# Two layers on one core: the second layer's dense weights load into the first layer's expert space, and its first sequence is entered in the first layer's last turns

## The chip, the core and the metric

The kernel runs on one core of a Trainium2 chip. The metric is the device time of one execution in microseconds (us); lower is better. Five engines work side by side, each with its own queue of instructions in a fixed order: TensorE (PE: matrix products and transposes; its weight loads are listed as PEld), VectorE (DVE), ScalarE (ACT), GpSimd (POOL) and SyncE (SP, which issues DMA transfers). ACT and POOL issue DMA transfers too. An instruction waits until the instructions whose results or buffers it needs are done, and everything behind it in its engine's queue waits with it.

## The reference

The input is 8 sequences of 512 tokens with 256 features, all in 32-bit floats. Cut to what matters here:

```python
xn = layernorm(x)
x = x + recurrent(xn) + experts0(xn)     # layer 0
xn = layernorm(x)
x = x + attention(xn) + experts1(xn)     # layer 1

# recurrent: mixes of neighbouring tokens, projections r, k, v, g, w; a forward and a
#   backward recurrence over the 512 tokens; sigmoid gate, group norm (16 heads), * silu(g), @ Wo
# experts0: each token goes to its 2 best of 8 experts (hidden size 704)
# attention: x + global_latent_attn(rmsnorm(x)), then + local_gqa_attn(rmsnorm(x)), window of 64
# experts1: 16 experts (hidden size 64): of 4 groups the best 2, of these the best 4 experts;
#   all experts are computed for all tokens and weighted; plus a shared expert of hidden size 512
```

The experts of layer 1 with the shared expert make 12 dense parts of 128 hidden units.

## The kernel before

The program is written as Python generators. A scheduler class, `Turns`, holds the running generators and advances each by one step per turn; a step ends at a `yield`. PE, DVE, ACT and SP execute their instructions in exactly the order in which this Python code issues them. Only POOL's order is chosen by the framework. So the order of everything around the change follows from how many `yield`s each generator has passed.

**Layer 0** (L239 to L808). After the norm, the routing and `place()` (slots of all tokens), the main loop is `scans`, in 64 turns over sequence, half of the features and group of values. For each group, DVE does one product (L688), four recurrences (L699, L703: two forward, two backward) and one product with r (L708), and PE sums over the keys (L714, `ys`). Beside `scans` run:

- `projections(b + 1)`, which prepares the next sequence.
- `ending(b, c, y, z, x)` for each finished half: gate (L734), centring product `yc` (L737), square (L740), variance (L747), root (L753, ACT), reciprocal (L755, DVE), widening (L758, ACT), transposes `rs` (L763, PE), z (L765, L766 on DVE, L767 on POOL); after the second half the output products `o` (L777), the sum x (L782) and the write of `after[b]` (L785, SP).
- `scatter`, then `experts`: 39 chunks of 256 slots. POOL fetches each chunk's weights; the results go to `outs` in DRAM (L472, L473).

The tiles of `experts` are in the pools `ew`, `h0` and `ex`; those of `projections`, `scans` and `ending` are in the pool `rw`; all of them close at the end of layer 0.

**Layer 1** (L811 to L1325) begins with the loads of all its weights on ACT's queue (L820 to L843; `w1` is the 12 dense parts, 384 KB each). Its own `Turns` then runs:

- `attentions`: 16 blocks in the order g0, g1, l0, g2, l1, ... (g is global, l is local attention; the number is the sequence). In each: scores (L1159, PE), exponential (L1167, ACT), mask (L1173, DVE), sums `o` (L1187, PE), and `divided` with the output projection. These give the turns.
- `heads_of(n)`: queries, keys and values of block n (L1001 to L1125), with rotary steps and norms on DVE.
- `entry(b)` (L891 to L994): loads `after[b]` into `acc`, gathers each token's two expert rows from `outs` (L903, POOL) and sums them (L911, DVE), norm (L919 to L926), transposes (L858), router logits (L945, PE), the choice of experts on DVE (L959 to L983, through `chosen`, L228 to L236), and the weights `cT` (L987), written to `cd` in DRAM.
- `ffn(b)` (L1254 to L1316): for each of 12 parts the products `g` and `u` (L1261, PE) and `h` (L1293 on ACT; L1296, L1279, L1281 on DVE; `cb` is a row of `cd`, loaded by SP), and after each six parts the products `y` (L1307). It starts once `entry(b)` is done.

The start of layer 1 in the kernel before:

```python
turns.add(
    then(*(heads_of(n) for n in range(len(BLOCKS)))),
    then(*(entry(b) for b in range(B))), then(*(ffn(b) for b in range(B))),
)
for _ in attentions(turns):
    turns.turn()
```

So `heads_of(0)` and `ffn(0)` wait for `entry(0)`, and the first score waits for `heads_of(0)`.

Of the kernel before, what the change touches and what calls it, by code (L numbers as in the profile page):

```python
# [26 lines left out]
F32 = mybir.dt.float32  # L27
# [9 lines left out]
P = 128  # L37
# [128 lines left out]
def two_layers(ctx: ExitStack, tc: tile.TileContext, a: dict, out: bass.AP):  # L166
# [6 lines left out]

    cst = const.tile([P, FIRST_L1], F32, name="cst")
# [6 lines left out]
    act_e.dma_start(wg0, a["wg0"])  # L181

# [38 lines left out]
    def chosen(dst, s, n, k, tri, tmp, tag, tags=None):  # L221

        rows = s.shape[1]
        tags = tags or (f"gt{n}", f"eq{n}")
        gt = tmp.tile([P, rows, n, n], F32, tag=tags[0], name=f"gt{n}_{tag}", bufs=1)
        eq = tmp.tile([P, rows, n, n], F32, tag=tags[1], name=f"eq{n}_{tag}", bufs=1)
        other, own = bc(s, 2, n), bc(s, 3, n)
        vec_e.tensor_tensor(gt, other, own, ALU.is_gt)  # L228
        vec_e.tensor_tensor(eq, other, own, ALU.is_equal)
        vec_e.tensor_tensor(  # L230
            eq.rearrange("p r i j -> p r (i j)"), eq.rearrange("p r i j -> p r (i j)"),
            bc(tri, 1, rows), ALU.mult,
        )
        vec_e.tensor_tensor(gt, gt, eq, ALU.add)
        vec_e.tensor_reduce(dst, gt, AX.X, ALU.add)
        vec_e.tensor_scalar(dst, dst, float(k), None, ALU.is_lt)  # L236


    with ExitStack() as l0:  # L239
# [3 lines left out]
        ew = l0.enter_context(tc.tile_pool(name="ew", bufs=2))  # L243
        hpool = l0.enter_context(tc.tile_pool(name="h0", bufs=4))
        ex = l0.enter_context(tc.tile_pool(name="ex", bufs=2))
# [20 lines left out]
        score = keep.tile([P, NTT, E0], F32, name="score")  # L266
        pick0 = keep.tile([P, NTT, E0], F32, name="pick0")
        slots = dram.tile([NSLOT, D], F32, name="slots", bufs=1)
        lines = [dram.tile([D, T], F32, name=f"xnT{b}", tag=f"xnT{b}", bufs=1) for b in range(B)]
        xns = [ex.tile([P, NT, D], F32, name=f"xn{b}", tag=f"xn{b}", bufs=1) for b in range(B)]  # L270

        def clear_slots():

            zero = rw.tile([P, D], F32, tag="t5a", name="zero")
            vec_e.memset(zero, 0.0)
            n = NSLOT // P
            nc.sync.dma_start(slots.rearrange("(p n) d -> p n d", p=P), bc(zero, 1, n))

        def norm_and_route(b):
# [25 lines left out]
            chosen(pick0[:, b * NT : (b + 1) * NT, :], s, E0, TOP0, C["tri8"], rw, f"a{b}")  # L305
# [499 lines left out]
        turns.add(then(scatter(), experts()))  # L805
# [5 lines left out]
    with ExitStack() as l1:  # L811
# [6 lines left out]
        dram = l1.enter_context(tc.tile_pool(name="dram1", bufs=3, space=DRAM))  # L818

        cst1 = keep.tile([P, NCONST - FIRST_L1], F32, name="cst1")  # L820
        act_e.dma_start(cst1, a["cst"][:, FIRST_L1:])
        for n, (lo, hi) in _C.items():
            if lo >= FIRST_L1:
                C[n] = cst1[:, lo - FIRST_L1 : hi - FIRST_L1]
        rtw = keep.tile([P, NC, E1], F32, name="rtw")
        act_e.dma_start(rtw, a["router_w"])
        cbias = keep.tile([P, E1], F32, name="cbias")
        act_e.dma_start(cbias, a["correction_bias"].to_broadcast([P, E1]))
        gq = keep.tile([P, NC, D], F32, name="gq")
        act_e.dma_start(gq, a["g_wq"])  # L830
# [4 lines left out]
        go = keep.tile([P, NC, D], F32, name="go")  # L835
        act_e.dma_start(go, a["g_wo"])
        lqkv = keep.tile([P, NC, D + P], F32, name="lqkv")
        act_e.dma_start(lqkv, a["l_wqkv"])
        lo_w = keep.tile([P, NC, D], F32, name="lo_w")
        act_e.dma_start(lo_w, a["l_wo"])  # L840
        w1 = [keep.tile([P, 3, D], F32, name=f"w1_{j}", tag=f"w1_{j}") for j in range(NF1)]
        for j in range(NF1):
            act_e.dma_start(w1[j], a["w1"][j])  # L843
# [8 lines left out]
        def transposed(src, name):  # L852

            out = []
            for c in range(NC):
                ps = bank(f"{name}{c}")
                for t in range(NT):
                    pe.transpose(  # L858
                        ps[:, t * P : (t + 1) * P], src[:, t, c * P : (c + 1) * P], ident
                    )  # L860
                out.append(ps)
            return out
# [20 lines left out]
        done = set()  # L883

        def until(*what):
            while what not in done:
                yield

        own = {}

        def entry(b):  # L891

            if b >= 3:
                yield from until("out", b - 3)
            acc = at.tile([P, NT, D], F32, tag="acc", name=f"acc{b}", bufs=3)
            nc.sync.dma_start(acc, tokens(after[b]))
            for half in range(2):
                ys = []
                for t in range(2 * half, 2 * half + 2):
                    n = b * NT + t  # L900
                    for i in range(2):
                        y = at.tile([P, D], F32, tag="y0", name=f"y0_{n}_{i}", bufs=4)
                        pool_e.indirect_dma_start(  # L903
                            out=y, out_offset=None, in_=outs,
                            in_offset=bass.IndirectOffsetOnAxis(ap=slot[i][:, n : n + 1], axis=0),
                        )
                        ys.append((t, n, i, y))
                yield
                yield
                for t, n, i, y in ys:  # L910
                    vec_e.scalar_tensor_tensor(  # L911
                        acc[:, t, :], y, wslot[i][:, n : n + 1], acc[:, t, :], ALU.mult, ALU.add
                    )
            yield
            x = at.tile([P, NT, D], F32, tag="x1", name=f"x1_{b}", bufs=3)
            st = small.tile([P, NT, 6], F32, tag="bnst", name=f"bnst_b{b}")
            mv = small.tile([P, NT, 2], F32, tag="bnmv", name=f"bnmv_b{b}")
            for t in range(NT):
                vec_e.bn_stats(st[:, t, :], acc[:, t, :])  # L919
                vec_e.bn_aggr(mv[:, t, :], st[:, t, :])  # L920
            rs = small.tile([P, NT], F32, tag="bnrs", name=f"bnrs_b{b}")
            vec_e.tensor_scalar(rs, mv[:, :, 1], 1e-05, None, ALU.add)
            rsqrt(rs, rs, NT)
            yield
            for t in range(NT):
                vec_e.tensor_scalar(  # L926
                    x[:, t, :], acc[:, t, :], mv[:, t, 0:1], rs[:, t : t + 1],
                    ALU.subtract, ALU.mult,
                )
            yield  # L930
            if b >= 2:
                yield from until("ffn", b - 2)
            pss = transposed(x, f"x_{b}")
            yield
            xT = at.tile([P, NC, T], F32, tag="xT", name=f"xT_{b}", bufs=2)
            for c in range(NC):
                act_e.copy(xT[:, c, :], pss[c])
            own[b] = acc, x, xT
            done.add(("x", b))
            yield  # L940

            ps = bank(f"lg_{b}")
            for t in range(NT):
                for c in range(NC):
                    pe.matmul(  # L945
                        ps[:, t * E1 : (t + 1) * E1], xT[:, c, t * P : (t + 1) * P], rtw[:, c, :],
                        start=c == 0, stop=c == NC - 1,
                    )
            yield


            def rt(n, tag):
                return at.tile([P, NT, n], F32, tag=tag, name=f"{tag}_{b}")

            s, sb, sel = rt(E1, "rs"), rt(E1, "rsb"), rt(E1, "rsel")
            gsel, gs = rt(G1, "rg"), rt(G1, "rgs")
            act_e.activation(s.rearrange("p n e -> p (n e)"), ps[:, : NT * E1], AF.Tanh, scale=0.5)
            yield
            vec_e.tensor_scalar(s, s, 0.5, 0.5, ALU.mult, ALU.add)  # L959
            vec_e.tensor_tensor(sb, s, bc(cbias, 1, NT), ALU.add)  # L960

            def groups(x):
                return x.rearrange("p n (g e) -> p (n g) e", g=G1)

            chosen(groups(sel), groups(sb), E1 // G1, 2, C["tri4"], at, f"g{b}")
            yield
            vec_e.tensor_tensor(sel, sel, sb, ALU.mult)
            vec_e.tensor_reduce(gs.rearrange("p n g -> p (n g)"), groups(sel), AX.X, ALU.add)
            chosen(gsel, gs, G1, 2, C["tri4"], at, f"h{b}")
            flat = gsel.rearrange("p n g -> p (n g)")  # L970
            vec_e.tensor_tensor(groups(sb), groups(sb), bc(flat, 2, E1 // G1), ALU.mult)
            vec_e.tensor_scalar(gsel, gsel, FMAX, FMAX, ALU.mult, ALU.subtract)
            vec_e.tensor_tensor(groups(sb), groups(sb), bc(flat, 2, E1 // G1), ALU.add)
            for t in range(0, NT, 2):
                yield
# [448 lines left out]
```

## Time and profile before

| | us |
|---|---|
| time, median of 3 runs | 2760.29 (2757.69 to 2765.39) |
| the profiled execution's own time | 2747.16 |
| its span | 2745.4 |
| PE busy | 2338.7 (85%) |
| DVE busy | 2141.9 (78%) |
| ACT busy | 865.9 (32%) |
| POOL busy | 472.3 (17%) |
| end of the last recurrence product (L708) | 1443.70 |
| first instruction of layer 1 | 1466.15 |
| first score product (L1159) | 1546.90 |

The span is the time from the first to the last instruction of the profiled execution; 1.8 us of its own time lie outside it. "Busy" is the time in which an engine executed something. In the timeline a line has the start in us, the duration in us, the engine, the line of the kernel, the operation, output<-inputs with shapes, and how many instructions are put together; in brackets stands how long the engine had been idle before and which engine's result, or which transfer, ended the idle time. In the waits the same idle times are summed by the instruction that waited.

### The profile page before, as it was taken

The page shows a single profiled execution, that of the slowest core. Times are in us where ns is not written, and L with a number is a line of the kernel's source. Part 1 is how long each engine was busy: PE and PEld are TensorE (multiplying, and loading weights), DVE is VectorE, ACT ScalarE, POOL GpSimd, SP SyncE. Part 2 cuts the span into 40 slices and gives each one's busy share as a digit, 9 for nine tenths or more (in the row PEclk, how much of TensorE's full clock was granted, in tenths as well). Part 3 has the DMA queues.
Part 4 walks back from the last instruction along what each step waited for, and adds up shares of the span by engine and source line. Part 5 has one row for each costly group of instructions (what it writes and reads, how often), then busy time and mean ns, then how long its engine had stood idle before and what let it go on. Part 6 is the DMA issues. An engine that isn't in the chain of part 4 may idle for free. (4 is left out here: it accounts for less than half of the span.)

```text
span 2745.4 us, 32489 instructions
## 1 busy us (share of the span) xinstructions
PE 2338.7 (85%) x11772; PEld 1392.8 (51%) x11772; DVE 2141.9 (78%) x3042; ACT 865.9 (32%) x1649; POOL 472.3 (17%) x446
## 2 busy tenths in 40 slices
PE   4756897998989889898864899999989989998996
PEld 3313555555555555555632445555545545555554
DVE  4698989989999999999994857667576676666666
ACT  1303231232312323132111344444333444334344
POOL 0075132222223222132202110010010101001000
PEclk8767998989999999998986999999989999999998
DMA  8245555445454454545533100010010111000000
GB/s 286 77 147 167 149 162 163 132 135 158 157 174 133 140 161 142 175 153 153 174 87 140 55 28 24 9 45 21 16 32 32 31 32 31 22 26 20 20 9 16
DMA packets 108912, 263.23 MB, mean 96 GB/s; under 512 B 25265, under 2 KB 56401, under 8 KB 103633
## 3 DMA queue, kind: packets, MB, share of 16 engines
q1 hardware_dynamic: 76304, 119.35, 15.1%
q0 software_dynamic: 23616, 124.14, 13.9%
q10 hardware_dynamic: 8832, 17.65, 1.7%
q8 instruction: 95, 1.56, 0.2%
q14 instruction: 65, 0.52, 0.1%
HBM read 215.17 MB, written 45.88 MB: 95 GB/s over the span
## 5 line engine op out<-in xcount | busy, mean ns | idle before, releaser
L703 DVE TENSOR_TENSOR_SCAN kv<-d,kv 128x512 f32<-128x512 f32 x256 | 336.9, 1316 | 8.8
L699 DVE TENSOR_TENSOR_SCAN kv<-dq,kv 128x512 f32<-128x512 f32 x256 | 324.8, 1269 | 2.5
L426 PE MATMUL g<-xsT,wgu 128*128 128x256 f32 x936 | 248.0, 412 | 20.1 <-ACT xsT L418 19.6
L465 PE MATMUL y<-wdn,h 128*128 128x256 f32 x936 | 254.5, 410 | 8.7 <-DVE h L435 8.7
L1167 ACT ACTIVATE pt_g<-sc_g 128x512 f32<-128x512 f32 (+1 forms) x384 | 171.0, 532 | 236.4 <-PE sc_g L1159 201.7
L426 PEld LDWEIGHTS g<-xsT,wgu 128*128 128x128 f32 x936 | 188.3, 206 | 102.1 <-issue 38.6
L465 PEld LDWEIGHTS y<-wdn,h 128*128 128x128 f32 x936 | 170.8, 197 | 105.2 <-issue 73.7
L1261 PE MATMUL g<-xT,w 128*128 128x512 f32 x384 | 197.5, 639 | 24.8 <-DVE h L1296 9.4
L1261 PE MATMUL u<-xT,w 128*128 128x512 f32 x384 | 190.7, 620 | 18.7 <-DVE h L1296 7.6
L714 PE MATMUL ys<-kv,cst 128*32 128x512 f32 x512 | 123.2, 653 | 79.0 <-DVE kv L708 78.8
L426 PE MATMUL u<-xsT,wgu 128*128 128x256 f32 x780 | 189.3, 382 | 0.0
L1307 PE MATMUL y<-w,h 128*128 128x256 f32 x768 | 179.3, 385 | 0.0
L426 PEld LDWEIGHTS u<-xsT,wgu 128*128 128x128 f32 x780 | 148.2, 191 | 36.2 <-issue 14.0
L708 DVE TENSOR_TENSOR kv<-kv,r 128x1024 f32<-128x1024 f32 x128 | 160.2, 1251 | 3.7
L1279 DVE TENSOR_TENSOR h<-h,u 128x512 f32<-128x512 f32 x96 | 66.0, 688 | 123.6 <-PE u L1261 119.0
L688 DVE TENSOR_TENSOR kv<-kv,k 128x1024 f32<-128x1024 f32 x128 | 160.2, 1251 | 0.0
L1307 PEld LDWEIGHTS y<-w,h 128*128 128x128 f32 x768 | 141.7, 190 | 32.2 <-issue 9.5
L452 ACT ACTIVATE h<-g 128x512 f32<-128x512 f32 (+1 forms) x117 | 61.5, 526 | 300.6 <-PE g L426 300.3
L1173 DVE TENSOR_TENSOR pt_g<-pt_g,cst 128x512 f32<-128x512 f32 x128 | 85.2, 686 | 69.7 <-ACT pt_g L1167 69.6
L1167 ACT ACTIVATE pt_l<-sc_l 128x384 f32<-128x384 f32 (+1 forms) x256 | 98.0, 470 | 90.9 <-PE sc_l L1159 72.9
L1261 PEld LDWEIGHTS g<-xT,w 128*128 128x128 f32 x384 | 71.4, 199 | 107.2 <-issue 82.6
L903 POOL DMA_INDIRECT y<-outs,slot x64 | 64.7, 1010 | 324.8 <-DVE acc L911 312.6
(298 smaller groups left out, 3858.9 us busy)
## 6 DMA issues: line engine op xcount, KB each, us to landing
kv<-vd SPq DMA_DIRECT2D x1024, 64.0 KB, 2.4
cb<-cd SPq DMA_DIRECT2D x128, 128.0 KB, 2.9
slots<-zero SPq DMA_DIRECT2D x1, 9984.0 KB
xs<-slots POOLq DMA_DIRECT2D x39, 256.0 KB, 7.2
outs<-ys POOLq DMA_DIRECT2D x39, 256.0 KB, 5.7
w<-in_w ACTq DMA_DIRECT2D x12, 384.0 KB, 9.7
xn<-in_x SPq DMA_DIRECT2D x8, 512.0 KB
xnT<-xT ACTq DMA_DIRECT2D x16, 256.0 KB, 2.0
```

The source lines that it names most:

```text
L426: pe.matmul(o, w[:, at + c * P : at + (c + 1) * P], xT[:, c, :], start=c == 0, stop=c == NC - 1,)
L465: pe.matmul(y[:, n, :], hs[j // 2][lo:, j % 2, n * P : (n + 1) * P], wd[lo:, j * D : (j + 1) * D], start=j == 0, stop=j == NJ0,)
L688: vec_e.tensor_tensor(kv, kv, bc(kc, 1, NV), ALU.mult)
L699: vec_e.tensor_tensor_scan(out=kv[:, i, :], data0=qc, data1=kv[:, i, :], initial=0.0, op0=ALU.mult, op1=ALU.add,)
L703: vec_e.tensor_tensor_scan(out=kv[:, i, ::-1], data0=dc[:, ::-1], data1=kv[:, i, ::-1], initial=0.0, op0=ALU.mult, op1=ALU.add,)
L708: vec_e.tensor_tensor(kv, kv, bc(rc, 1, NV), ALU.mult)
L714: pe.matmul(y[r0 : r0 + 32, :], C["take"][:, 24 - 8 * at : 56 - 8 * at], kv[:, i, :], start=at == 0, stop=at == 3, skip_group_check=True,)
L1167: act_e.activation(pt[:, i, :end], scs[i][:, :end], AF.Exp, scale=0.25)
L1173: vec_e.tensor_tensor(pt[:, :, a0 : a0 + m], pt[:, :, a0 : a0 + m], bc(mask[:, :m], 1, 4), ALU.mult,)
L1261: pe.matmul(ps, w[:, k, c * P : (c + 1) * P], xT[:, c, :], start=c == 0, stop=c == NC - 1,)
L1279: vec_e.tensor_tensor(hs[-1], hs[-1], u, ALU.mult)
L1307: pe.matmul(y[:, i, :], hs[k][:, (t + i) * P : (t + i + 1) * P], w1[j - 5 + k][:, 2, :], start=k == 0, stop=k == 5,)
```

## The change

The generator `entry` and its helpers `transposed` and `until` move ahead of both layers, so that they can run in either; they take their PSUM banks and temporary tiles from a dictionary, `place_of`, that each layer fills. A pool `hold` of eight tiles is shared by the layers: in layer 0 they hold the eight normed sequences, in layer 1 the tiles `acc`, `x1` and `xT` of `entry`. The pools of the experts go to the right side of the memory and are closed when the last chunk is done. Then a new generator, `begin`, opens a pool of the dense weights in that place, loads three small tables, starts `entry(0)` in layer 0's turns, and after six turns loads `gq`, `go`, `lqkv` and the 12 dense parts, one per turn. `entry(0)` uses tiles of `rw` and banks of `ps_gu` there. Layer 1 loads only what is left (`cst1`, `gdown`, `gup`, `lo_w`) and starts with `entry(1)`. Cut to its core:

```diff
+    hold = ctx.enter_context(tc.tile_pool(name="hold", bufs=1))
+    def held(i, shape, name):
+        return hold.tile(shape, F32, tag=f"held{i}", name=name)
...
+    def entry(b):
+        if b >= 3:
+            yield from until("out", b - 3)
+        bank, temp = place_of["bank"], place_of["temp"]
+        acc = held(b % 3, [P, NT, D], f"acc{b}")
...
-        xns = [ex.tile([P, NT, D], F32, name=f"xn{b}", tag=f"xn{b}", bufs=1) for b in range(B)]
+        xns = [held(b, [P, NT, D], f"xn{b}") for b in range(B)]
...
-        turns.add(then(scatter(), experts()))
+        def begin():
+            side.close()
+            pool = ctx.enter_context(tc.tile_pool(name="w1", bufs=1, side="right"))
+            yield
+            act_e.dma_start(cstr, a["cst"][:, first1:last1])
+            act_e.dma_start(rtw, a["router_w"])
+            act_e.dma_start(cbias, a["correction_bias"].to_broadcast([P, E1]))
...
+            turns.add(entry(0))
+            for _ in range(6):
+                yield
+            for name, of, shape in (
+                ("gq", "g_wq", [P, NC, D]), ("go", "g_wo", [P, NC, D]),
+                ("lqkv", "l_wqkv", [P, NC, D + P]),
+            ):
+                W[name] = pool.tile(shape, F32, name=name)
+                act_e.dma_start(W[name], a[of])
+                yield
+            for j in range(NF1):
+                w1.append(pool.tile([P, 3, D], F32, name=f"w1_{j}", tag=f"w1_{j}"))
+                act_e.dma_start(w1[j], a["w1"][j])
+                yield
+        W, w1 = {}, []
+        def last():
+            turns.add(begin())
+            yield
+        slot_work = then(scatter(), experts(), last())
+        turns.add(slot_work)
         for _ in scans(turns):
             turns.turn()
         turns.finish()
...
-        w1 = [keep.tile([P, 3, D], F32, name=f"w1_{j}", tag=f"w1_{j}") for j in range(NF1)]
-        for j in range(NF1):
-            act_e.dma_start(w1[j], a["w1"][j])
...
-            then(*(entry(b) for b in range(B))), then(*(ffn(b) for b in range(B))),
+            then(*(entry(b) for b in range(1, B))), then(*(ffn(b) for b in range(B))),
```

## The prediction, made before the result was known

> **What bounds the kernel now.** I read the slices first, to see which engine carries which stretch:
>
> ```profile
> ## 2 busy tenths in 40 slices
> PE   4756897998989889898864899999989989998996
> DVE  4698989989999999999994857667576676666666
> ...
> PEclk8767998989999999998986999999989999999998
> ```
>
> The span has two halves. Up to about 1445 us VectorE is the full engine (the scans); from about 1550 us TensorE is. The change works at the seam, which the windows of 20 us take apart (columns: start:end, length, busy time of PE, PEld, DVE, ACT and POOL, the granted clock, DMA share, GB/s):
>
> ```profile
> 1420.00:1440.00 20.00, 5.93 (x14) 0.52 (x12) 19.62 (x18) 0.59 (x1) 0.77 (x1) 0.55 0.03 13
> 1440.00:1460.00 20.00, 10.77 (x26) 5.58 (x26) 6.59 (x9) 3.26 (x5) 1.25 (x1) 0.51 0.00 0
> 1460.00:1480.00 20.00, 1.99 (x8) 1.44 (x8) 2.63 (x5) 0.00 (x0) 8.99 (x12) 0.66 0.68 231
> 1480.00:1500.00 20.00, 8.83 (x28) 5.79 (x28) 10.33 (x29) 3.64 (x5) 7.14 (x8) 0.50 0.67 251
> 1500.00:1520.00 20.00, 13.84 (x40) 7.30 (x40) 17.60 (x41) 5.95 (x12) 0.00 (x0) 0.82 0.10 28
> 1520.00:1540.00 20.00, 12.85 (x40) 6.36 (x40) 17.28 (x41) 3.33 (x6) 9.66 (x9) 0.87 0.31 93
> 1540.00:1560.00 20.00, 19.67 (x83) 9.43 (x82) 12.97 (x34) 8.65 (x17) 1.00 (x1) 0.96 0.21 67
> ```
>
> No engine is full from 1440 to 1500. In that hole lie layer 0's last ending, a chain of short steps, and the wait for gathers that share the DMA engines with 250 GB/s of weights. The timeline of VectorE shows both:
>
> ```profile
> 1442.47 1.23 DVE L708 TENSOR_TENSOR kv<-kv,r 128x1024 f32<-128x1024 f32 x1
> ...
> 1451.45 0.35 DVE L755 RECIPROCAL sd<-sd 128x32 f32<-128x32 f32 x1 [5.05 <-ACT sd L753]
> 1453.67 0.69 DVE L765 TENSOR_TENSOR z<-z,rs 128x512 f32<-128x512 f32 x1 [1.86 <-PE rs L763]
> ...
> 1462.08 0.69 DVE L782 TENSOR_TENSOR x<-x,o 128x512 f32<-128x512 f32 x1 [2.09 <-PE o L777]
> ...
> 1476.04 1.56 DVE L911 SCALAR_TENSOR_TENSOR acc<-y,wslot,acc 128x256 f32<-128x256 f32 x3 [13.27 <-DMA y<-outs,slot]
> ...
> 1486.44 0.48 DVE L911 SCALAR_TENSOR_TENSOR acc<-y,wslot,acc 128x256 f32<-128x256 f32 x1 [0.79 <-DMA y<-outs,slot]
> ```
>
> The scans end at 1443.70, the last x at 1462.77, and the first score product of layer 1 starts at 1546.90, 84.1 us later. Of these, 24 pass before sequence 0's sums are complete (1486.9).
>
> **The change, part by part** (times of the profiled execution, 2747.16 us; line numbers of the kernel before). No arithmetic is added or removed. One constants load becomes two. The order of instructions follows from the built program, so what I estimate is only where each waits.
>
> *A. Layer 0's tail gets longer.* Between the last scans VectorE now executes eight L911 sums (8 x 0.48 = 3.8), the statistics and x of sequence 0 (2.45 + 1.38 = 3.8), and waits for the second four gathers: they reuse the first four's buffers, start when those are summed, are issued 1.27 apart and land 3.40 later (row at 1526.40), about 2.2 too late. L708 ends 9.8 later, at 1453.5. On TensorE the x transposes (2.27) precede the last ys, and the logits (3.18, 0.5 of it inside the wait for yg) precede yc: +2.7. The reciprocal L755 stands behind the router's first part, 9.2 us on VectorE (1497.32 to 1506.50); the norm's chain alone would bring it there 12.5 later, the router at 17.0 later: +4.5. z L765 stands behind the second part (3.6 + 1.1), of which the 1.86 of waiting for rs covers its share: +2.8. Sum: the last x at 1482.6 instead of 1462.77, **+19.8**. Queues passed: POOL gets eight gathers and one power ahead of the last z (8 x 1.27 + 1.0, some 11 us, done before VectorE asks); SP gets two acc loads ahead of the write of after; ACT gets 15 loads, about 0.8 us of issue each (the twelve dense loads take 9.84 now), one in each turn between sd and wide, where VectorE's router part is later anyway. Without that cover each costs its 0.8. The cb loads of the first dense part queue on SP behind the write of after and land 2.9 after it, before h_0 asks for them (B: 11.1).
>
> *B. Layer 1's opening gets shorter.* After the last x nothing can start for 3.4 us (1462.77 to 1466.15: the write's issue and the release of layer 0's space). Then sequence 1's first four gathers: issued within 3.8, landing 3.4 later, summed 0.5: 11.1 after the last x. h_0 (three VectorE rows of 0.69, 2.1) to 13.2; the second four gathers, summed to 17; the second product's u and h_1 to 22. From there VectorE works through a fixed row: the rotary and norm steps of block g0 (1.49 + 1.55 + 1.49 + 1.49 + 2.84 + 1.2 + 1.42 + 1.28 = 12.8), sequence 1's statistics, x and router (2.45 + 1.38 + 2.88 + 2.6 + 7.27 + 1.15 = 17.7), h_2 to h_5 (8.4): 38.9. Then TensorE's cT (1.0) and a y group (2.8) stand ahead of the first score. 22 + 38.9 + 3.8 = 64.7 against 84.1: **-19.4**.
>
> A and B cancel (+0.4): the first score comes at the same moment. What differs is what TensorE has done by then.
>
> *C. Work done ahead.* By the first score three more dense products (g or u, 1.98 each: 5.9), three more y groups (2.76 each: 8.3), sequence 1's logits (1.96) and cT (0.60) are behind. As TensorE is nearly full afterwards (324 of 340 us from 1560 to 1900), that is time off the end: **-16.8**.
>
> *D. One more gap without dense work.* Counted in score instructions, the dense parts of sequences 0 to 3 ran at 0-76, 76-184, 184-280, 288-384; now at 0-52, 52-152, 152-252, 280-380. From the 408th on nothing changes. So a gap of 28 score instructions, in which attention has no dense product to fill its waits, now lies also ahead of the fourth; before it was 8. Such a gap later in the trace shows its price on TensorE:
>
> ```profile
> 2205.68 1.65 PE L1187 MATMUL o_l<-pt_l,va_l 128*32 128x192 f32 x16 [2.97 <-DVE pt_l L1173]
> 2207.26 1.66 PE L1159 MATMUL sc_l<-qkT_l,qkT_l 32*128 32x192 f32 x16
> 2211.24 1.02 PE L987 MATMUL cT<-cst,rsel 128*16 128x128 f32 x4 [2.31 <-DVE rsel L983]
> 2212.05 1.92 PE L1051 MATMUL qkv_g<-gq,xg_g 128*128 128x256 f32 x4
> ```
>
> Idle 2.97 + 2.31 = 5.3, and behind each wait rows at about half speed (o_l 1.65, elsewhere 0.75; cT 1.02 against 0.60; sc_l 1.66 against 0.83; qkv 1.92 against 1.13): 2.9 more, 8.2 in all (10.0 in the gap at 2045). I take 8.2, the same block at the same place; ends 5.3 and 10.0. Against that, the period from the fourth cT to the fifth (1891.43 to 2054.91: 163.5, less 5.65 of y groups that the others have elsewhere) is 1.5 over the steady 156.3; these stalls go: **+6.7**.
>
> [...]
>
> Sum: 19.8 - 19.4 - 16.8 + 6.7 = **-9.7**: 2737.5 in the profiled execution. The median of the three runs is 13.13 higher (2760.29), so **2750.6**. About 0.3% (8.3 us, so 2752.0 to 2768.6) is what a measurement can tell from no change: the forecast lies just beyond it.
>
> **Unknown costs.** The gathers that now run without weights may land in 3.4 (row at 1526.40) or in 7.2 (row at 1468.20, with weight traffic). In A the weights start only later and in B only four small loads are left, so I take 3.4; the other end costs 3.8 in each of four waves of four, 15.2, less about 2 of slack in the first: up to +13. A stall at 1586.7 (3.13 of idle, then g rows of 3.37 and 1.59 more idle, 6.1 together) belongs to the opening and may go: down to -6.1.
>
> **Rivals.**
> 1. *Larger gain.* The 1586 stall goes and D is at its lower end: 2750.6 - 6.1 - 2.9 = 2741.6.
> 2. *Late gathers*, +13: 2763.6. For it: all sixteen gathers of sequences 0 and 1 are followed by sums behind which VectorE's other work queues. Against it: the landing of 3.40, and 13 to 28 GB/s in the windows where they will run.
> 3. *The lead is worth nothing: slower.* If from the first score on the attention's own chain (score, exp on ACT, mask on VectorE, o) sets the pace and dense products only fill its waits, the 16.8 done ahead leave holes instead of shortening anything: +0.4 + 8.2, 2768.9, up to 2780 if other gaps grow too. Against it: TensorE idles only 20.5 of the 440 us from 1600 to 2040. For it: the gaps without dense work are short of nothing else. It decides once TensorE's idle time after the first score grows by over 16.8.
> 4. *The clock stays low in the opening: slower.* The rows from 1420 to 1500 show .50 to .66. Some 47 us of TensorE work at full rate lie in B (13.84 + 12.85 + 7 in the windows from 1500 to 1547, plus C, less 3.2 of logits that are now in the tail); at half rate they are 94, more than VectorE's 64.7, and up to 29 come on top: about 2780. Against it: .82 and .87 as soon as dense products come (1500 to 1540).
> That the change does nothing is excluded: entry 0's instructions stand between the last scans.
>
> **How the numbers follow.** Forecast (2743 to 2757: D's ends, three quarters of the 1586 stall, a third of the late landing): .44, of which .29 is faster by over 0.3% and .15 within it. Rival 1 .16, faster. Rival 2 .14, within. Rival 3 .18, of which .13 slower and .05 within. Rival 4 .08, slower. Faster .45, same .34, slower .21. The range from 2736 (rival 1 less the 5.3 that D still costs in it) to 2773 (rival 3's middle) leaves about .2 out. Forecast and rival 1 alone: 2738 to 2757.
>
> **What would show it.** A: the last L708 at about 1453.5, the reciprocal at 1468, the last x at 1482.6. B: no load of dense weights after it, the first score near 1547. C: twelve g and u products and three y groups ahead of that score, instead of nine and none, and the last product of the first dense part some 17 us earlier. D: idle of about 3 + 2.3 with slow rows ahead of the fourth dense part. The prediction is wrong if the last x comes after 1495, if the first score comes after 1560, or if TensorE's idle time from there to 2060 grows by more than 15.

## The result, and the profile after

The change makes the kernel slightly slower: 2766.86 us (median of 20 runs, 2755.15 to 2777.63) against 2757.78 (20 runs beside them), ratio 1.003 with a 95% interval of 1.002 to 1.004. The forecast was 2750.6, faster. The profiled execution after has its own time of 2768.28 us and a span of 2766.5.

The slices of the page after:

```profile
## 2 busy tenths in 40 slices
PE   4756898988989899898864899998989989998996
...
DVE  4698989999999998999986766566676675656656
...
PEclk8768998999999899999986999999999999999998
```

In the slice from 1452 to 1521 TensorE still has its 4; VectorE has 6 where it had 4. The windows of 20 us at the seam, with the same columns as before the change:

```profile
1420.00:1440.00 20.00, 10.84 (x36) 5.25 (x36) 18.31 (x18) 0.59 (x1) 3.17 (x4) 0.82 0.22 73
1440.00:1460.00 20.00, 0.65 (x2) 0.00 (x0) 10.76 (x13) 0.00 (x0) 6.14 (x6) 0.50 0.56 161
1460.00:1480.00 20.00, 7.72 (x42) 4.73 (x42) 14.52 (x34) 4.04 (x7) 2.19 (x2) 0.66 0.26 83
1480.00:1500.00 20.00, 8.93 (x28) 5.29 (x28) 12.25 (x30) 1.19 (x2) 2.80 (x2) 0.66 0.46 150
1500.00:1520.00 20.00, 12.26 (x26) 5.28 (x27) 8.50 (x16) 5.06 (x8) 12.87 (x18) 0.74 0.60 173
1520.00:1540.00 20.00, 18.25 (x64) 9.53 (x63) 15.42 (x30) 6.33 (x13) 2.99 (x2) 1.00 0.15 46
```

The hole of before is filled only in part (TensorE 7.72 and 8.93 of 20 us from 1460 to 1500), and a new one lies ahead of it: from 1440 to 1460, still among the scans, VectorE is busy for only 10.76 of 20 us. VectorE's timeline after names it (L833, L853, L293, L900, L910 and L927 are the L688, L708, L911, L755, L765 and L782 of before):

```profile
1437.45 1.23 DVE L853 TENSOR_TENSOR kv<-kv,r 128x1024 f32<-128x1024 f32 x1
1447.92 1.23 DVE L833 TENSOR_TENSOR kv<-kv,k 128x1024 f32<-128x1024 f32 x1 [9.25 <-DMA kv<-vd]
...
1462.26 0.48 DVE L293 SCALAR_TENSOR_TENSOR acc<-y,wslot,acc 128x256 f32<-128x256 f32 x1 [0.95 <-DMA y<-outs,slot]
...
1471.04 1.22 DVE L853 TENSOR_TENSOR kv<-kv,r 128x1024 f32<-128x1024 f32 x1
...
1485.39 0.34 DVE L900 RECIPROCAL sd<-sd 128x32 f32<-128x32 f32 x1
...
1490.37 0.68 DVE L910 TENSOR_TENSOR z<-z,rs 128x512 f32<-128x512 f32 x1
...
1498.45 0.69 DVE L927 TENSOR_TENSOR x<-x,o 128x512 f32<-128x512 f32 x1 [2.09 <-PE o L922]
```

The last but one group of scans waits 9.25 us for its kv rows, which SP loads. The answer on SP's own queue (waits from 1404 to 1450; columns: line, what it waited for, us in total, times, longest) tells why they were late:

```profile
SPq L810 <- DMA cstr<-in_cst: 13.6, 1, 13.6
SPq L810 <- PE ys L859: 11.4, 2, 8.3
SPq L810 <- DMA kv<-vd: 5.3, 3, 2.6
SPq L810 <- DMA lqkv<-in_l_wqkv: 3.0, 1, 3.0
SPq L810 <- DMA gq<-in_g_wq: 2.7, 1, 2.7
```

SP's issue of a kv row waited 13.6 us for a table of layer 1 to land, later ones 2.7 for gq and 3.0 for lqkv, although no kv row depends on them. The last of the group's eight rows was issued at 1443.18; VectorE, which needs all eight, went on at 1447.92.

All later comparisons count from the end of the fourth-last L708 (L853 after), because up to there all kernels below execute the same instructions in the same order (but for three small loads at the start of some), and single profiles still reach it up to 18 us apart (1421.8 before, 1440.0 in one of the experiments). Before's profile was the earliest of all. From there on, in us:

| kernel | scans (to the end of the last L708) | ending (to the last x) | opening (to the first score) | rest (to the end of the span) | sum against before | ratio to before, 95% interval |
|---|---|---|---|---|---|---|
| before | 21.9 | 19.1 | 84.1 | 1198.5 | | |
| forecast | 31.7 | 29.1 | 64.7 | 1188.4 | -9.7 | |
| after | 40.9 | 26.9 | 70.5 | 1196.9 | +11.6 | 1.003, 1.002 to 1.004 |
| e1_late_weights | 31.5 | 29.2 | 68.3 | 1196.0 | +1.3 | 1.0006, 0.9987 to 1.0024 |
| e2_weights_only | 32.4 | 19.2 | 77.8 | 1197.6 | +3.4 | 1.0015, 0.9999 to 1.0032 |
| e3_entry_only | 31.5 | 30.9 | 83.5 | 1196.1 | +18.4 | 1.0074, 1.0046 to 1.0102 |
| e4_late_weights_only | 24.2 | 19.2 | 80.1 | 1195.9 | -4.1 | 0.9989, 0.997 to 1.0008 |
| h2_pool_loads | 39.3 | 28.7 | 70.3 | 1196.7 | +11.4 | one run |
| g1_less_y | 21.9 | 20.9 | 83.1 | 1188.5 | -9.2 | 0.9966, 0.9953 to 0.9979 |
| f1_entry_in_waits | 21.9 | 19.0 | 59.8 | 1200.4 | -22.4 | 0.9926, 0.9911 to 0.9941 |
| f2_split_weights | 21.9 | 19.0 | 58.6 | 1205.1 | -19.0 | 0.9912, 0.9891 to 0.9933 |

A ratio of 1.003 is 8 us, so the sums of single profiles and the timed ratios tell the same story, to within some 5 us. h2_pool_loads has one run, so its line is that of one profile alone.

### The profile page after: what moved, and what is told of

Its sections match the earlier page's. It is cut to its first block, busy times and chain, and to the rows that moved or that the text cites. A ratio compares the mean times of both kernels' runs of the same rounds, so it can differ in the third digit from the quotient of the medians.

```text
span 2766.5 us, 32493 instructions
## 1 busy us (share of the span) xinstructions
PE 2355.5 (85%) x11772; PEld 1397.9 (51%) x11772; DVE 2143.0 (77%) x3042; ACT 868.0 (31%) x1649; POOL 470.4 (17%) x446
## 4 chain that ended last, share of the span: by engine, by line
PE 53%; DVE 26%; issue 7%; DMA 7%; ACT 4%; SPq 1%; POOL 1%; another core or an unknown queue 0%; DVEq 0%; ACTq 0%; POOLq 0%
PE y L1359 6%; PE g L571 5%; PE g L1313 5%; PE u L1313 4%; DMA kv<-vd 4%; PE u L571 4%; DVE kv L844 3%; DVE kv L848 3%; PE y L610 3%; PE sc_g L1211 2%; PE ys L859 2%; PE o_g L1239 2%; PE qkv_l L1103 2%; SPq L810 1%; PE qkv_g L1103 1%
## 5 line engine op out<-in xcount | busy, mean ns | idle before, releaser
L1313 PE MATMUL g<-xT,w 128*128 128x512 f32 x384 | 203.3, 655 | 27.3 <-DVE att_l L1267 14.0
L833 DVE TENSOR_TENSOR kv<-kv,k 128x1024 f32<-128x1024 f32 x128 | 160.2, 1252 | 9.2 <-DMA kv<-vd 9.2
L853 DVE TENSOR_TENSOR kv<-kv,r 128x1024 f32<-128x1024 f32 x128 | 160.2, 1251 | 3.6
L1225 DVE TENSOR_TENSOR pt_l<-pt_l,cst 128x768 f32<-128x768 f32 (+1 forms) x128 | 107.9, 885 | 12.7 <-ACT pt_l L1219 12.7
```

The costliest lines, as they stand in the source:

```text
L833: vec_e.tensor_tensor(kv, kv, bc(kc, 1, NV), ALU.mult)
L853: vec_e.tensor_tensor(kv, kv, bc(rc, 1, NV), ALU.mult)
L1225: vec_e.tensor_tensor(pt[:, :, a0 : a0 + m], pt[:, :, a0 : a0 + m], bc(mask[:, :m], 1, 4), ALU.mult,)
L1313: pe.matmul(ps, w[:, k, c * P : (c + 1) * P], xT[:, c, :], start=c == 0, stop=c == NC - 1,)
```

## The experiments

Two theories of the tail stood against each other. The *queue theory*: SP's kv loads queue behind the completion of ACT's weight loads. The *order theory*: entry 0's own steps between the scans cost the time, and the loads are free.

**e1_late_weights.** The small tables at the kernel's start, the dense weights behind the last kv loads:

```diff
     cbias = const.tile([P, E1], F32, name="cbias")
+    act_e.dma_start(cstr, a["cst"][:, first1:last1])
+    act_e.dma_start(rtw, a["router_w"])
+    act_e.dma_start(cbias, a["correction_bias"].to_broadcast([P, E1]))
...
-            for _ in range(6):
+            for _ in range(10):
                 yield
             for name, of, shape in (
```

> As the changed kernel, but the three small tables load at the kernel's start, and the dense weights only behind the last kv loads of the scans. Queue theory (the kv loads of the last two groups of scans stood on SP behind the completion of weight loads that ACT had issued: VectorE idle 9.25 us before L833): that idle time goes, L853 of the last group and the last x come about 9 earlier against the group before them, and the time falls from 2766.9 to about 2757.5. Order theory (it is entry 0's own work between the last scans that costs; the loads are free): the idle time is taken up by something else and the time stays at 2767.

The 9.25 us are gone: the scans take 31.5 instead of 40.9, and the kv row of the last but one group is there (no idle time before this L836, the L833 of after):

```profile
1446.06 1.22 DVE L856 TENSOR_TENSOR kv<-kv,r 128x1024 f32<-128x1024 f32 x1
1447.20 1.25 DVE L836 TENSOR_TENSOR kv<-kv,k 128x1024 f32<-128x1024 f32 x1
```

2.3 of it come back in the ending (29.2 instead of 26.9). In the changed kernel TensorE's granted clock (PEclk in the windows) was 1.00 from 1474.0 to 1479.0, and the logits took 1.96 us; before, where the window from 1480 to 1500 has 0.50, 14 of the 16 logits products took 3.17. VectorE waited 3.1 us for the router's ACT step behind the logits in e1, 1.42 in the changed kernel. That e1's logits ran at the lower clock is an estimate from these numbers. The time is 1.0006 of before. The queue theory holds for this part. What remains, 31.5 against 21.9 and 29.2 against 19.1, is entry 0's own work, and within 0.2 us what the prediction had computed for it (31.7 and 29.1).

**h2_pool_loads.** The early loads issued by POOL instead of ACT, all else as in the changed kernel:

```diff
-            act_e.dma_start(cstr, a["cst"][:, first1:last1])
+            pool_e.dma_start(cstr, a["cst"][:, first1:last1])
...
-                act_e.dma_start(w1[j], a["w1"][j])
+                pool_e.dma_start(w1[j], a["w1"][j])
```

> The changed kernel with the early loads (tables, gq, go, lqkv, dense parts) issued by POOL instead of ACT, at the same turns. Completion theory (SP's kv loads wait because they share completion counters with ACT's weight loads, whatever the bandwidth): no idle time before the last two L833 and the 127th group's last L708 7.3 after the 126th's (plus 1.9 of sums). Bandwidth rival (kv loads are late because weights fill the DMA engines): the idle time of 9 us before L833 stays. In both, the second four gathers stand on POOL behind the weight loads, so the sums in the last group wait longer than the 2.7 us in all of the changed kernel; the total time says little.

No idle time before either L833, and the group takes 9.0 (7.3 and the sums). On SP's queue only waits for PE and DVE are left (14.6 and 2.7 us). In exchange the second four gathers stand on POOL behind the weights, and VectorE waits there:

```profile
1441.34 1.26 DVE L833 TENSOR_TENSOR kv<-kv,k 128x1024 f32<-128x1024 f32 x1
...
1461.98 1.92 DVE L293 SCALAR_TENSOR_TENSOR acc<-y,wslot,acc 128x256 f32<-128x256 f32 x4 [10.41 <-DMA y<-outs,slot]
```

So in both runs the same loads held up other transfers: issued by ACT, kv rows (SP waited 13.6 us, VectorE 9.25); issued by POOL, the gathers behind them in its queue (VectorE waited 10.41). The bandwidth rival is not closed by h2: POOL's weight loads started only at 1443.5, after the last kv row was issued (1431), so the two were not in flight together. The changed kernel's own trace decides most of it. The 13.6 us were a wait for a 136 KB table that ACT had not yet issued (it stood behind the copy of the last ys, at 1431.4), and without SP's waits all rows would have been issued ahead of the first weight load (gq, at 1436.36). But the last row, once issued, took 4.7 us until VectorE went on, where the median kv row of before lands in 2.4 after its issue. So about 2 of the 9.25 us (an estimate from these two) can be traffic, and that only because the rows were late.

**e2_weights_only** and **e3_entry_only** do one half of the change each. e2 takes the early entry out:

```diff
-            turns.add(entry(0))
...
-            then(*(entry(b) for b in range(1, B))), then(*(ffn(b) for b in range(B))),
+            then(*(entry(b) for b in range(B))), then(*(ffn(b) for b in range(B))),
```

> Only the loads of tables and weights are early, as in the changed kernel; entry 0 runs in layer 1 as before. Queue theory: the last scans lose the same 9 us to the kv loads, the opening wins about 6 because its gathers land without weight traffic (3.4 instead of 7.2): about 2761. Order theory: no loss in the scans, only the 6 won: about 2752.

The scans lose 10.5 (VectorE again idle for 10.4 us before one L833), the opening wins 6.4. The queue theory's 2761 was 3 above before; the measured ratio of 1.0015 is 4 above.

e3 keeps entry 0 early, with the tables loaded at the start, and moves the weight loads to layer 1:

```diff
+        pool = place_of["w1"]
+        for name, of, shape in (
...
+            W[name] = pool.tile(shape, F32, name=name)
+            act_e.dma_start(W[name], a[of])
+        for j in range(NF1):
+            w1.append(pool.tile([P, 3, D], F32, name=f"w1_{j}", tag=f"w1_{j}"))
+            act_e.dma_start(w1[j], a["w1"][j])
         gq, go, lqkv = W["gq"], W["go"], W["lqkv"]
```

> Only entry 0 is early (tables loaded at the start); the dense weights load at the start of layer 1 as before. Queue theory: no idle time before the last L833 (-9), but the opening's gathers and first products wait for weight traffic again (+8): about 2766. Order theory: 2767 plus that 8: about 2775.

1.0074 is 20 us slower than before. The queue theory's 2766 was too low; the order theory's 2775 (a ratio of 1.0062) lies in the interval, but not for its reason: the scans are those of e1, without the idle time, and it is the opening that takes 83.5. ACT issued the twelve dense parts from 1498.13 to 1514.61, and the first square of layer 1, at 1517.20, stands behind them (waits of e3's opening, 1497 to 1580):

```profile
ACT sq_g L1070 <- DMA w<-in_w: 29.3, 1, 29.3
...
DVE rms_g L1027 <- ACT sq_g L1070: 14.7, 1, 14.7
```

Before, entry 0's 24 us of gathers and sums covered those loads (the twelve were issued by 1484.2, the first square ran at 1493.70); with entry 0 early, nothing does. The early loading is thus not an addition to the early entry but its condition.

**e4_late_weights_only** puts both edits of e1 and the edit of e2 together: late weights, entry 0 in layer 1.

> Weights behind the last kv loads, in layer 0's last ending; entry 0 in layer 1 as before. Both theories: layer 0's tail as before (last x about 19 after the last L853), the opening's gathers land in about 3.4 instead of 7.2, first score about 78 after the last x instead of 84: about 2752, faster than the kernel before by 6.

The ending is as before (19.2), the opening 80.1 instead of the expected 78, and 2.2 us of waiting for a kv row remain, since gq still came before that row in the order of the loads (SP waited 15.4 us for it). Ratio 0.9989, an interval that holds 1: about half of the expected 6.

**g1_less_y.** Is TensorE work that is taken out of the stretch after the first score time off the end? This is the kernel before with 4 of 6 terms left out of the first y products of sequences 0 to 3:

```diff
-                            for k in range(6):
+                            for k in (range(6) if j > 5 or b > 3 else (0, 5)):
```

> The kernel before, with part of the computation left out: in the first six dense parts of sequences 0 to 3 each y product sums only two of its six terms, which removes 4 x 7.5 = 30 us of TensorE work, all of it after the first score, with the order of everything else kept. TensorE-bound theory (as the prediction's term C had it: TensorE work taken out of this stretch is time off the end): 30 faster, ratio 0.989. Rival (the attention's chain or VectorE sets the pace, dense work fills waits): less than 10 faster, ratio above 0.996.

9 us of 30. The windows from the first score to the cT of the fifth sequence's entry, before and in g1:

```profile
1546.90:2054.91 508.01, 476.91 (x2954) 272.54 (x2953) 337.74 (x662) 208.26 (x447) 37.38 (x46) 0.98 0.08 26
```

```profile
1558.97:2054.89 495.92, 455.80 (x2825) 250.36 (x2825) 337.68 (x662) 208.14 (x447) 37.53 (x46) 0.97 0.09 27
```

Some 30 us fewer products (an estimate, 7.5 for each sequence) make TensorE's busy time only 21.1 shorter (what is left runs slower, clock 0.97 instead of 0.98), its idle time 9.0 longer, and the stretch 12.1 shorter. TensorE is 94% busy here and still not the bound by itself.

**f1_entry_in_waits.** e1 left the cost of entry 0's own steps. Whether it is a matter of their place, f1 tests: it gathers all eight row sets first and puts the sums, statistics and x of entry 0 into the ending's waits; its router goes back to layer 1:

```diff
+        if b == 0:
+            ys = []
+            for t in range(NT):
+                pair = temp([P, 2, D], "y0", f"y0_{t}", 4)
...
+            for _ in range(LAG[0]):
+                yield
+            for t, i, pair in ys:
+                vec_e.scalar_tensor_tensor(
...
+                if t % 2 and i:
+                    yield
...
-            then(*(entry(b) for b in range(1, B))), then(*(ffn(b) for b in range(B))),
+            then(route(0), *(then(entry(b), route(b)) for b in range(1, B))), then(*(ffn(b) for b in range(B))),
```

Here `LAG` is (8, 3, 1): eight turns before the sums, three more before x, one more before the transposes; `route` is `entry` from the logits on. The tables load at the start, and `begin` waits 12 turns instead of 6 before the dense weights.

> Entry 0 up to its transposed copy stays in layer 0, but its VectorE steps lie in the waits of the last ending instead of between the scans (all eight gathers first, then the sums before and after yg, the statistics before the reciprocal, x after it); the router of entry 0 goes back to layer 1; tables load at the start, dense weights behind the last kv loads. The order in layer 1 from the first xg on is that of the kernel before. Placement theory (the costs measured in the tail come from where entry's steps stand in VectorE's and TensorE's queues and from the kv loads behind weight loads; the work itself fits into waits): scans as before (21.9 from the fourth-last to the last L708), last x about 20 after the last scan, first score about 58 to 62 after the last x instead of 84, the rest 1196 to 1198 as in all runs so far: 20 to 24 faster than the kernel before, about 2737. Rival (whatever the entry saves at the opening comes back in the tail, or the first score is held by gathers and weights): the sum from the fourth-last L708 to the first score stays within 5 of 125, about 2755.

The ending of f1 on VectorE (here L297 are the sums, L326 and L327 the statistics, L335 is x):

```profile
1459.69 1.91 DVE L297 SCALAR_TENSOR_TENSOR acc<-y,wslot,acc 128x256 f32<-128x256 f32 x4
1461.79 0.69 DVE L912 TENSOR_TENSOR yg<-sig,ys 128x512 f32<-128x512 f32 x1 [0.19 <-PE ys L892]
1462.39 1.91 DVE L297 SCALAR_TENSOR_TENSOR acc<-y,wslot,acc 128x256 f32<-128x256 f32 x4
...
1467.53 0.35 DVE L933 RECIPROCAL sd<-sd 128x32 f32<-128x32 f32 x1 [0.87 <-ACT sd L931]
1467.82 1.38 DVE L335 TENSOR_SCALAR x<-acc,bnmv_b,bnrs_b 128x256 f32<-128x256 f32 x4
1469.90 0.69 DVE L943 TENSOR_TENSOR z<-z,rs 128x512 f32<-128x512 f32 x1 [0.70 <-PE rs L941]
...
1478.08 0.69 DVE L960 TENSOR_TENSOR x<-x,o 128x512 f32<-128x512 f32 x1 [2.82 <-PE o L955]
1486.32 0.88 DVE L1106 TENSOR_SCALAR xg_g<-xT,vecs 128x512 f32<-128x512 f32 x2 [7.56 <-DMA after<-x]
```

The idle times of before (2.03, 5.05, 1.86) have shrunk to 0.19, 0.87 and 0.70; the ending has its 19.0 us as before, and the part of entry 0 that is left in layer 0 costs nothing there. Its router is no longer in the tail, so f1 does not show that the router could hide there too. The late weights are not the gain: alone (e4) they brought 4 us, f1 brings 22. The first score comes 59.8 after the last x. 2738.04 us against 2757.22, ratio 0.9926: the placement theory's 2737.

**f2_split_weights.** f1's last row waits 7.56 us for the write of the last x, beside 360 GB/s of weights (the mean from 1470 to 1480). f2 loads eight of the twelve dense parts at layer 1's start:

```diff
-                act_e.dma_start(w1[j], a["w1"][j])
-                yield
+                if j < 4:
+                    act_e.dma_start(w1[j], a["w1"][j])
+                    yield
...
         act_e.dma_start(lo_w, a["l_wo"])
+        for j in range(4, NF1):
+            act_e.dma_start(w1[j], a["w1"][j])
```

> As f1_entry_in_waits, but only four of the twelve dense parts load in the ending, the other eight at layer 1's start. Traffic theory (in f1 the write of after took until 7.6 us past the last x because 360 GB/s of weights ran beside it): the write lands in about 3.4, the first xg comes 4 earlier, the first score 55 to 56 after the last x, 4 faster than f1, ratio to the kernel before about 0.991. Rival (what is saved there is lost to the gathers of sequence 1 and the first products behind the eight late loads): first score 60 or more after the last x, ratio 0.9926 or above.

The wait falls from 7.56 to 4.32, the way the traffic theory says, though not to its 3.4 (ACT issued the eight late loads from 1472.78 on, inside the wait), and 2.8 us of waiting come back right behind it, for the square on ACT, which stands behind the eight late loads:

```profile
1475.57 1.11 DVE L1109 TENSOR_SCALAR xg_g<-xT,vecs 128x512 f32<-128x512 f32 x2 [4.32 <-DMA after<-x]
1479.51 1.22 DVE L1064 TENSOR_REDUCE rms_g<-sq_g 128x4 f32<-128x1024 f32 x1 [2.83 <-ACT sq_g L1107]
```

The first score comes 58.6 after the last x, between the two theories. In f2's profile the rest is 4.6 longer than f1's, which no run explains. 0.9912 and 0.9926 overlap in their intervals: whether f2 beats f1 stays open.

## Why the prediction was wrong

*A, the tail: one queue was missed.* The forecast's +19.8 consisted of +9.8 in the scans and +10.0 in the ending. Measured: +19.0 and +7.8. The scans' +9.8 was right (e1 without the waiting: +9.6); the 9.25 us for kv rows come on top. The ending's parts were right as well (in e1 the reciprocal comes 7.3 later, forecast 2.7 + 4.5, and z another 2.8); that the changed kernel's ending grew by 7.8 only goes with the clock of 1.00 named at e1, which the prediction did not foresee.

The prediction had listed the 15 loads as issue time on ACT, "one in each turn between sd and wide, where VectorE's router part is later anyway". In the trace gq, go, lqkv and the first dense part were issued from 1436.36 to 1437.70, among the last scans, and the three tables at 1431.4. The failing step is that it looked at the queue in which the loads stand, put them too late there, and did not look at those that wait for their completion; it had that wait at nothing. The trace of the changed kernel shows the link: each issue has the number of the semaphore that its landing raises and of those that it waits for. From 1404 to 1450 the issues of SP and ACT take eight of them in turn (100 and 102 to 108), and each waits first for the number that it raises itself. The table issued at 1431.40 and the kv row issued at 1433.49 both have 100, which the table's landing raised for the last time at 1433.48; gq has 105 and lqkv 108, like the rows issued at 1438.95 and 1443.18. What stood behind the waiting row on SP waited with it: between the row of 1419.57 and that of 1433.49 SP issued nothing. The last x came 36.4 later than before in the two traces, 26.8 from the common point, not 19.8.

*B, the opening: right in kind, 5.7 short.* -13.7 instead of -19.4. The release after the last x took 4.4 instead of 3.4 (VectorE waited for the write of after). The first gather of sequence 1 was issued 5.0 after the last x instead of 3.4, the sums of the first four began 4.1 to 4.7 after their issue, where 3.4 had been taken (beside 173 GB/s from 1500 to 1520, where the prediction had counted on 13 to 28), so the wave was summed at 13.6 instead of 11.1, and h_1 was done at 25.5 instead of 22. So the mis-sized terms are the release, the landing of the gathers (rival 2, at a fraction of its price) and h_1 behind them. The row of VectorE work behind it was 2.3 longer than computed (45.0 to the first score, forecast 42.7).

*C and D, the lead: the premise failed.* The forecast took 10.1 off the rest; measured are 1.6 (1198.5 to 1196.9). The kernels with the lead (after, e1, e3, h2) have a rest of 1196.0 to 1196.9, those of the same order without it (before, e2, e4) 1195.9 to 1198.5: the lead, less the new gap, was worth nothing that these runs can tell. The lead itself was there: twelve g and u products and three y groups stand ahead of the first score, as forecast. On TensorE, D came as computed, 2.98 and 2.32 of idle time with slow rows behind them; what it cost in time no run isolates. The new gap ahead of the fourth dense part shows the predicted pair of waits:

```profile
1911.51 1.64 PE L1239 MATMUL o_l<-pt_l,va_l 128*32 128x192 f32 x16 [2.98 <-DVE pt_l L1225]
1913.08 1.66 PE L1211 MATMUL sc_l<-qkT_l,qkT_l 32*128 32x192 f32 x16
1917.07 1.02 PE L369 MATMUL cT<-cst,rsel 128*16 128x128 f32 x4 [2.32 <-DVE rsel L365]
```

C failed, in the step "As TensorE is nearly full afterwards ... that is time off the end". From the first score to the cT of the fifth entry TensorE's busy time is 8.7 shorter after the change, D's slow rows included, and its idle time 5.4 longer. New waits have come up, the longest 5.37 us, where a transpose of the attention waits on TensorE for VectorE's queue, which works through the choice of experts (7.3 us) in front of h:

```profile
1669.63 0.66 PE L1262 MATMUL oq_g<-cst,oT_g 128*128 128x128 f32 x2 [5.37 <-DVE h L1348]
```

g1 shows the same without any change of order: of 30 us of TensorE work about a third is time. This was rival 3's mechanism, at .18; its point of decision, an idle time grown by 16.8, was set too high, since slower rows swallowed work as well as idle time did (in g1 some 9 of the 30 us, an estimate: busy time fell by 21.1). That the measured time lies near rival 3's 2768.9 is luck all the same: rival 3 had A and B at +0.4 together, and they measured +13.1.

The range (2736 to 2773) held the time; the sign of the forecast was wrong. The three misses add up: 9.25 less 2.2 in A, 5.7 in B, 8.5 in C and D make 21.3, which turns -9.7 into the +11.6 of the profile; none of them alone turns the sign. Of the prediction's own signs of being wrong two came, the last x at 1499.1 (limit 1495) and the first score at 1569.6 (limit 1560); but 9.6 of both lie ahead of the common point, and counted from there they are at 1489.6 and 1560.0.

## What to carry to other kernels

A transfer that is moved must be followed to three places: the queue that issues it, the transfers that wait for the same semaphore, and whatever waits behind those. Here kv rows on SP stood 13.6, 2.7 and 3.0 us behind loads of ACT, and VectorE 9.25 behind the rows. Work that was brought forward was free only in a wait that already existed: entry 0's sums, statistics and x cost 9.6 us between the scans (e1 against before) and nothing inside the ending's idle times (f1); the router behind them cost most of another 10.1 in the ending. And a busy share of 94% did not make TensorE's work time (in g1 9 of some 30 us, an estimate): leave some of it out and measure before a lead on that engine is counted.

## What the runs showed of the hardware

The granted clock fell within a pause of 2.98 us in the gap above: it was 0.50 in the windows from 1911.4 to 1920 (0.89 in the 3.4 us ahead, the pause included; if it went from 1 to 0.50 once, that was some 2 us into the pause, an estimate from the 0.89), and the rows behind ran at half speed, as the windows of that stretch show (after the change):

```profile
1908.00:1911.40 3.40, 0.53 (x4) 0.28 (x4) 3.26 (x7) 1.20 (x4) 0.00 (x0) 0.89 0.00 0
1911.40:1914.70 3.30, 3.19 (x32) 1.59 (x32) 3.23 (x5) 0.00 (x0) 0.00 (x0) 0.50 0.00 0
...
1917.00:1920.00 3.00, 2.93 (x9) 1.87 (x10) 2.96 (x7) 0.57 (x1) 0.00 (x0) 0.50 0.06 16
```

A shorter pause, of 2.33 us up to 1798.87, left the clock at 1.00 (windows from 1796.5 to 1802).

Single executions of one program differ by 15 to 25 us (before: 2750.7 to 2765.39 over 20 runs; e4_late_weights_only: 2743.63 to 2768.52 over 12), and between the ten profiles the part that all kernels share differs by up to 18 us. A seam of 10 us can be read from one profile only when it is counted from an instruction behind that part.
